# Three edits in one: tokens kept on chip and a split first norm in layer 0, five row blocks of layer 1's convolution on VectorE, and a regrouped softmax, selection and scatter in the experts

## The chip, the cores and the metric

The kernel runs on one core of a Trainium2 chip. The metric is the device time of one execution in microseconds (us). The engines are PE (TensorE), DVE (VectorE), ACT (ScalarE), POOL (GpSimd) and SP (SyncE), which issues all of this kernel's DMAs. Each engine works through its own instructions in program order, and waits on semaphores for the others.

## The reference, cut to what matters

The input `x` is [2, 56, 56, 128] in float32: two images (b) of 3136 tokens with 128 channels. Four layers follow one another.

```
x = x + ss2d0(groupnorm(x))            # layer 0: in_proj, 3x3 depthwise conv, SiLU, four selective scans, norm * SiLU(z), out_proj
x = four_heads(x)                      # layer 1: per head of 32 channels: layernorm, in_proj, 3x3 conv, SiLU,
                                       #   four selective scans, gated norm, out_proj; a head starts from the sum
                                       #   of the head before and its own chunk; then a final layernorm
t = t + attention(ln(t))               # layer 2
t = t + spectral_mixer(ln(t))
t = t + attention(ln(t))               # layer 3
t = t + experts(ln(t))

def experts(x):                        # 64 experts, K = 8 tokens for each expert and image
    probs = softmax(x @ gate_w.T + gate_b, axis=tokens)
    topv, topi = top_k(probs, 8)                   # per expert, along the tokens
    pooled = sum_k topv * x[topi]                  # one row for each expert
    h = gelu([pooled, 1] @ weight1)
    o = [h, 1] @ weight2
    out.at[topi].add(topv * o)                     # scattered back to the tokens
```

A depthwise convolution has nine taps for each channel, and each output row needs the row above and the row below.

## The kernel before, in words

The tokens are 28 blocks of 112 (`TP`, `NT`). `k.X` [112, 28, 2, 128] is the running activation, and stays in SBUF for the whole program. Channels lie in partitions in chunks of `CH` = 448 tokens (eight image rows), so there are seven chunks (`NCH`). Six large buffers `big` are used in turn by all layers; `pair` in the profile holds the first two, which layer 0 calls `y[0]` and `y[1]`.

**Layer 0** (`layer0`). Nine weight loads stand first in SP's queue. `norm(b)` (L574) loads the tokens of an image into a tile `xt` (L580), transposes them on PE (L99, in groups of four), evacuates by DVE and ACT in turn (L64, L68), takes statistics (L587, L589), sums over groups of four channels with a matmul by `grp` (L591, L598) and normalises (L603). The result is stored to DRAM in `kept` (L604). Both images are normalised before anything else. Then, for each image b, a loop over c = 0..7 calls `before`: chunk c of the norm is loaded back (`hin`, L645), projected on PE (L648) into zero-bordered images `pad0` and `pad1` (L649 on ACT), and the convolution of chunk c-1 is made by `conv_rows`. That has two forms: on PE as nine matmuls with diagonal matrices `diag` (L460, 18 instructions in the profile), or on DVE as one multiplication and eight multiply-adds (L464, L466). ACT applies SiLU (L467), and POOL writes a transposed copy (L468). Channel half 1 is always on DVE; half 0 is on PE except for c = 2 and 5. At c = 2, `scans.first` prepares the first group of the scan (projections L166, the step `keep` that stores its rows at L182, `fetch` of `whole` at L189, `spread` of `three` at L205); its two scratch areas lie in `y[0]` and `y[1]`. After the loop `scans.run` works through 512 scan steps per image. In the scan stages the order of the instructions is written out by hand; in all other stages a scheduler orders them and places the waits.

**Layer 1** (`Layer1`). Between two scans there is a transition: `after` closes a head, `before` opens the next for the same chunk c: `layernorm_tokens`, four transposes, projection (L844 into `pad`, L856 for the gate), convolution of chunk c-1 (c = 2, 4, 6 on DVE; 1, 3, 5, 7 on PE), gate. The first transition (from about 2769 us to 2914 us) has layer 0's `after` beside it; the three others follow each head. The PSUM pool `pcon1` has two buffers, which projections and PE convolutions share. The first step of the new scan needs `b` (a matmul by L364), `h` (L417 on DVE) and `a` (L339 on ACT).

**Experts** (`Experts.run`). `pr` holds the logits, experts of both images in the 128 partitions and tokens along the free dimension. DVE finds the eight largest (L1785), and marks them in a copy `sel` (L1788, match_replace). ACT takes the exponential with its sum (L1789), and scales by the reciprocal (L1791); DVE makes `sel` the probabilities at the marks and zero elsewhere (L1792). PE transposes `sel` (L1797), DVE multiplies by the layernorm's scale (L1801), and 56 matmuls pool the tokens (L1805). After the 64 experts (L1837, L1847, L1828) `oe` is bias plus outputs (L1868, L1869), and for each image and each four token blocks four matmuls with 64 rows scatter it back (L1876), DVE adds `X` into `xo` (L1881, three buffers), and SP stores it (L1882).

Of the kernel before, what the change touches and what calls it, by code (L numbers as in the profile page):

```python
# [21 lines left out]
B = 2  # L22
# [536 lines left out]
def layer0(k, d, big, follow):  # L559
# [3 lines left out]
    with ExitStack() as ctx:  # L563
        wp = ctx.enter_context(k.pool("w0"))
        W = {n: load(nc, wp, d["L0_" + n], "L0" + n) for n in (
            "in_w", "in_b", "taps", "conv_b", "dtb", "A", "Ds", "onw", "onb")}
        negative_exp(nc, W["A"])
# [6 lines left out]
        def norm(b, pools, G):  # L574

            ip, pp = pools
            hT = ip.tile([128, L], F32, name="hT")
            xt = ip.tile([TP, NT, C], F32, name="xt")
            for j in range(0, NT, 4):
                nc.sync.dma_start(  # L580
                    xt[:, j : j + 4], d["x"][b, TP * j : TP * (j + 4)].rearrange("(j p) c -> p j c", p=TP)
                )
            tokens_to_channels(k, pp, lambda c0: hT[:, c0 : c0 + CH], lambda j: xt[:, j, :])
# [22 lines left out]
        with ExitStack() as sctx:  # L606
# [11 lines left out]
            with k.pool("in0", 2) as ip, k.pool("pin0", 2, psum=True) as pp:  # L618

                grp = ip.tile([128, 32, 4], F32, name="grp0")  # L620
                nc.vector.tensor_reduce(grp[:, :, 0], k.ident.rearrange("p (g c) -> p g c", c=4), AX.X, ALU.add)
                nc.vector.tensor_scalar_mul(grp[:, :, 0], grp[:, :, 0], 0.25)
                for c in range(1, 4):
                    nc.vector.tensor_copy(grp[:, :, c], grp[:, :, 0])
                for b in range(B):
                    norm(b, (ip, pp), grp.rearrange("p g c -> p (g c)"))
# [13 lines left out]
            def before(b, pools, c, pads, diag):  # L640

                sp, pp = pools
                if c < NCH:
                    h = sp.tile([128, CH], F32, name="hin")
                    nc.sync.dma_start(h, kept[b, :, CH * c : CH * (c + 1)])  # L645
# [7 lines left out]
                if c > 0:  # L653
                    for ci in range(2):
                        conv_rows(
                            k, pools, pads[ci], diag, W["taps"][:, ci], W["conv_b"][:, ci : ci + 1], row[ci],
                            col[ci], c - 1, "DVE" if ci == 1 or c in (2, 5) else "PE",
                        )
# [41 lines left out]
            for b in range(B):  # L700
                with ExitStack() as bctx:
# [8 lines left out]
                    diagonals(k, diag, W["taps"][:, 0])  # L710
                    for ci in range(2):
                        pads.append(ip.tile([128, PAD, PAD], F32, name=f"pad{ci}"))
                        clear_border(nc, pads[ci])
                    for c in range(NCH + 1):
                        if b > 0 and c < NCH:
                            after(b - 1, (sp, pp, ip), c, *outs)
# [16 lines left out]
class Layer1:  # L733
# [85 lines left out]
    def before(self, head, pools, c, pad):  # L819
# [29 lines left out]
        if c > 0:  # L849
            conv_rows(  # L850
                k, (sp, vp), pad, self.diag, W["taps"], W["conv_b"], self.row, self.col, c - 1,
                "DVE" if c % 2 == 0 else "PE",
# [852 lines left out]
class Experts:  # L1705
# [6 lines left out]

    NE, NH, EC = 64, 512, 4
# [51 lines left out]
    def run(self, out):  # L1765
        k, nc, tc, X, W = self.k, self.k.nc, self.k.tc, self.k.X, self.W
        NE, NH, EC, pr = self.NE, self.NH, self.EC, self.pr
        with ExitStack() as ctx:
# [14 lines left out]
            with k.pool("e3t") as up, k.pool("pe3", 2, psum=True) as pp:  # L1783
                top = up.tile([128, 8], F32, name="top")
                nc.vector.max(top, self.tops.rearrange("p c n -> p (c n)"))  # L1785
                m = up.tile([128, 3], F32, name="m")
                nc.vector.tensor_scalar_mul(m[:, 0:1], top[:, 0:1], -1.0)
                nc.vector.match_replace(sel, top, pr, -3e38)  # L1788
                nc.scalar.activation(pr, pr, AF.Exp, bias=m[:, 0:1], accum_out=m[:, 1:2])  # L1789
                nc.vector.reciprocal(m[:, 2:3], m[:, 1:2])  # L1790
                nc.scalar.activation(pr, pr, AF.Copy, scale=m[:, 2:3])  # L1791
                nc.vector.scalar_tensor_tensor(sel, sel, -2e38, pr, ALU.is_lt, ALU.mult)  # L1792
                selT = up.tile([TP, NT, B, NE], F32, name="selT")
                for j in range(0, NT, 4):
                    ps = pp.tile([TP, 4, B, NE], F32, name="ps")
                    for i in range(4):
                        nc.tensor.transpose(  # L1797
                            ps[:, i].rearrange("p b e -> p (b e)"), sel[:, TP * (j + i) : TP * (j + i + 1)], k.ident
# [3 lines left out]
                ps = pp.tile([128, B, NE], F32, name="pp")  # L1802
                for b in range(B):
                    for j in range(NT):
                        nc.tensor.matmul(  # L1805
                            ps[:, b], lhsT=X[:, j, b, :], rhs=selT[:, j, b], start=j == 0, stop=j == NT - 1
                        )
                raw = up.tile([128, B, NE], F32, name="raw")
                nc.vector.tensor_copy(raw, ps)
                ps = pp.tile([128, B, NE], F32, name="pp")  # L1810
                nc.tensor.matmul(ps, lhsT=less, rhs=raw, start=True, stop=True)
                for b in range(B):
                    for e in range(EC):
                        k.evacuate(pooled[:, e::EC, 2 * e + b], ps[:, b, e::EC])
# [47 lines left out]
            oe = sp.tile([128, C], F32, name="oe")  # L1862
# [5 lines left out]
            nc.vector.tensor_copy(oe, pb)  # L1868
            nc.vector.tensor_tensor(oe, oe, every, ALU.add)  # L1869
            op = ctx.enter_context(k.pool("e3o", 3))  # L1870
            po = ctx.enter_context(k.pool("peo", 2, psum=True))
            for b in range(B):
                for j in range(0, NT, 4):
                    ps = po.tile([TP, 4, C], F32, name="po")
                    for i in range(4):
                        nc.tensor.matmul(  # L1876
                            ps[:, i, :], lhsT=sel[NE * b : NE * (b + 1), TP * (j + i) : TP * (j + i + 1)],
# [142 lines left out]
```

## Time and profile before

| what | before |
|---|---|
| median of three runs (all runs) | 9146.21 us (9146.21, 9135.08, 9156.23) |
| profiled execution: its time, its span | 9148.52 us, 9146.7 us |
| busy, share of the span | PE 88%, DVE 77%, POOL 69%, ACT 42% |
| mean granted TensorE clock | 0.947 |
| first scan instruction of layer 0, image 0 | 115.83 us |
| transitions into layer 1's heads 0 and 1: first scan instruction | 2914.59 us, 3648.01 us |
| experts: start of match_replace, last pooling matmul's result read | 8958.63 us, 8991.62 us |
| last scatter addition starts | 9142.44 us |

A line of the timeline has the start in us from the span's start, the duration in us, the engine, the line in the code, the operation, the tiles written and read with their shapes, and how many instructions are merged; in brackets stand the idle time before it and what ended it. A line of windows has, for a stretch of time, the busy time and the number of instructions of each engine, the granted clock of PE (1.00 is full speed) and the share and rate of the DMA engines. A PE matmul in float32 counts as two instructions, a PE transposition as one.

### The profile page before, as it was taken

The numbers are of one execution on the slowest core, as the hardware profiler recorded it, in microseconds if no ns is written. First come the engines' busy times: TensorE is split into PE (matmuls) and PEld (weight loads), VectorE is DVE, ScalarE is ACT, GpSimd is POOL, SyncE is SP. The second block draws the span as 40 slices with busy tenths as digits, with TensorE's granted clock in tenths as the row PEclk, the third lists the DMA queues.
The fourth block names the chain that finished last, engine by engine and source line by source line (L and its number), as shares of the span: only waits on it lengthen the run. The fifth ranks groups of instructions, "written<-read, shape, count | busy, mean of one in ns | idle before, by whom it ended". The sixth has DMA issues, their size and how long they took to land.

```text
span 9146.7 us, 93661 instructions
## 1 busy us (share of the span) xinstructions
PE 8045.3 (88%) x28769; PEld 4798.2 (52%) x28769; DVE 7065.7 (77%) x7533; ACT 3851.1 (42%) x6642; POOL 6343.6 (69%) x4065
## 2 busy tenths in 40 slices
PE   7888888888888888888888888699999999999998
PEld 3444445444445444444444444455688888874555
DVE  8999998999996997998899799611467677665442
ACT  4555555555555554554554555433211111114331
POOL 5999996999995997998899799566311111115551
PEclk9999999999998998998999899799999999999998
DMA  5666663676663995996788599100233333320003
GB/s 154 222 219 220 223 219 123 219 221 222 221 223 93 227 229 135 224 228 163 193 228 213 146 227 228 43 3 3 85 96 104 103 95 109 91 62 7 14 5 129
DMA packets 781377, 1364.55 MB, mean 149 GB/s; under 512 B 133213, under 2 KB 406494, under 8 KB 780842
## 3 DMA queue, kind: packets, MB, share of 16 engines
q1 hardware_dynamic: 780874, 1358.56, 52.8%
q8 instruction: 228, 3.74, 0.2%
q14 instruction: 275, 2.25, 0.1%
HBM read 1318.63 MB, written 39.60 MB: 148 GB/s over the span
## 4 chain that ended last, share of the span: by engine, by line
PE 46%; DVE 26%; issue 14%; ACT 7%; POOL 4%; DMA 2%; SPq 1%; DVEq 0%; POOLq 0%; ACTq 0%
DVE h L358 13%; PE cv L1548 13%; DVE h L417 8%; PE av L1059 6%; PE sc L1065 5%; PE acc L378 4%; PE pj L1662 4%; ACT a L339 3%; PE b L166 3%; PE pcv L460 2%; DMA c<-rows 1%; PE b L364 1%; POOL p L430 1%; POOL h L433 1%; PE acc L392 1%
## 5 line engine op out<-in xcount | busy, mean ns | idle before, releaser
L430 POOL TENSOR_TENSOR p<-h,c 128x784 f32<-128x784 f32 x2048 | 3754.3, 1856 | 115.9 <-DVE h L358 37.8
L358 DVE TENSOR_TENSOR_SCAN h<-a,state,h 128x784 f32<-128x784 f32 x1536 | 2788.3, 1837 | 48.6 <-ACT a L339 26.8
L378 PE MATMUL acc<-p,center 128*128 128x392 f32 x4096 | 1500.8, 500 | 16.0 <-POOL p L430 14.9
L378 PE MATMUL acc<-p,ident 128*128 128x392 f32 x4096 | 1494.3, 499 | 6.1 <-POOL p L430 6.0
L417 DVE TENSOR_TENSOR h<-du,b 128x784 f32<-128x784 f32 x1408 | 1332.5, 946 | 86.2 <-PE b L364 81.0
L339 ACT ACTIVATE a<-delta,L0A 128x784 f32<-128x784 f32 x1024 | 939.1, 918 | 974.3 <-DVE h L358 972.1
L339 ACT ACTIVATE a<-delta,L1A 128x784 f32<-128x784 f32 x1024 | 939.2, 917 | 911.9 <-DVE h L358 908.7
L364 PE MATMUL b<-three,sel 96*128 96x512 bf16 (+1 forms) x2816 | 730.4, 342 | 561.1 <-DVE h L417 456.6
L433 POOL TENSOR_TENSOR h<-du,b 128x784 f32<-128x784 f32 x640 | 1185.8, 1853 | 9.7 <-PE pcv L460 9.7
L378 PEld LDWEIGHTS acc<-p,center 128*128 128x128 f32 x4096 | 742.9, 193 | 529.3 <-POOL p L430 50.7
L378 PEld LDWEIGHTS acc<-p,ident 128*128 128x128 f32 x4096 | 745.4, 193 | 512.7 <-issue 26.8
L1078 POOL TENSOR_TENSOR total<-total,e 128x448 f32<-128x448 f32 (+1 forms) x644 | 735.6, 1142 | 325.1 <-ACT e L1067 285.7
L364 PEld LDWEIGHTS <-sel 96*128 96x128 bf16 x2816 | 282.1, 100 | 1231.9 <-issue 1052.9
L358 DVE TENSOR_TENSOR_SCAN h<-a,h 128x784 f32<-128x784 f32 x512 | 900.6, 1777 | 33.6 <-ACT a L339 23.2
L1561 DVE TENSOR_TENSOR u<-u,cv 128x512 f32<-128x512 f32 x1024 | 623.3, 679 | 326.8 <-PE cv L1548 325.5
L1592 POOL TENSOR_TENSOR u<-u,S 128x1024 f32<-128x1024 f32 x64 | 150.0, 2366 | 1042.7 <-DVE S L1561 1042.7
L1067 ACT ACTIVATE e<-sc 128x448 f32<-128x448 f32 (+1 forms) x700 | 377.4, 543 | 725.4 <-PE sc L1065 592.8
L1563 ACT COPY u<-cv 128x512 f32<-128x512 f32 x256 | 149.5, 587 | 827.2 <-PE cv L1548 773.5
L1662 PE MATMUL pj<-u,Wm 128*128 128x196 f32 (+8 forms) x1536 | 354.3, 384 | 5.7 <-DVE A L1668 5.7
L1065 PE MATMUL sc<-big 128*128 128x448 f32 (+1 forms) x700 | 323.2, 547 | 15.2 <-ACT e L1067 12.1
L1059 PE MATMUL av<-e,big 128*128 128x448 f32 (+1 forms) x700 | 320.8, 545 | 1.1 <-DVE e L1072 1.0
L1642 POOL TENSOR_TENSOR both<-mpm 128x512 f32<-128x512 f32 x32 | 40.6, 1270 | 391.2 <-DVE Wm L1698 271.7
(449 smaller groups left out, 11289.0 us busy)
## 6 DMA issues: line engine op xcount, KB each, us to landing
c<-rows SPq DMA_DIRECT2D x1024, 392.0 KB, 4.1
c<-rows SPq DMA_DIRECT2D x2048, 196.0 KB, 4.8
b<-rows SPq DMA_DIRECT2D x320, 392.0 KB, 4.6
b<-rows SPq DMA_DIRECT2D x640, 196.0 KB, 4.5
H<-raw SPq DMA_DIRECT2D x32, 1568.0 KB, 7.6
wC<-win SPq DMA_DIRECT2D x64, 576.0 KB, 6.3
w<-in_L_weight_dram SPq DMA_DIRECT2D x52, 512.0 KB, 5.6
wA<-win SPq DMA_DIRECT2D x64, 384.0 KB, 5.5
```

The lines of the kernel that those rows point to most:

```text
L339: self.k.nc.scalar.activation(x["a"], g["delta"][ci], AF.Exp, scale=self.w["A"](g["kd"], ci, x["n"]))
L358: self.k.nc.vector.tensor_tensor_scan(h, a, h, start, ALU.mult, ALU.add)
L364: self.k.nc.tensor.matmul(ps[:, c0:c1], lhsT=self.w["selB"](x["n"]), rhs=x["g"]["three"][:, c0:c1], start=True, stop=True)
L378: nc.tensor.matmul(job["acc"][:, i, 0:392], lhsT=self.w["sum"], rhs=x["p"][:, 392 * i : 392 * (i + 1)], start=False, stop=n == NS - 1,)
L417: nc.vector.tensor_tensor(one["h"], one["g"]["du"][one["ci"]], one["b"], ALU.mult)
L430: nc.gpsimd.tensor_tensor(now["p"], now["h"], now["c"], ALU.mult)
L433: nc.gpsimd.tensor_tensor(three["h"], three["g"]["du"][three["ci"]], three["b"], ALU.mult)
L1059: nc.tensor.matmul(acc, lhsT=V[b][:n, j, :], rhs=e[:n], start=j == 0, stop=j == NKT - 1)
L1065: nc.tensor.matmul(ps[:n], lhsT=keys[b][:, KT * j : KT * j + n], rhs=q, start=True, stop=True)
L1078: nc.gpsimd.tensor_tensor(total[:n], total[:n], e[:n], ALU.add)
L1548: self.k.nc.tensor.matmul(ps[:, b], lhsT=v[:, C * b : C * (b + 1)], rhs=h, start=i == 0, stop=i == len(terms) - 1)
L1662: nc.tensor.matmul(ps[:, lo - c0 : hi - c0], lhsT=Ws[f][:, eo, r, :], rhs=u[:, b, f, lo - a0 : hi - a0], start=f == 0, stop=f == 1,)
```

## The change

Layer 0: the tokens of image 0 are loaded straight into `X` ahead of the weights, those of image 1 after the weights. `norm` writes to `y[b]` instead of a tile of its own. Image 0's norm runs at the start of its loop, and its chunks are read from `y[0]` without the load; image 1's norm is called inside that loop at c = 2. `kept` is stored for both, as before. The convolution of half 0 of image 0 is on PE for all chunks; for image 1 it stays as it was. The diagonals are made after the pads.

Layer 1: the convolutions on DVE are those of c = 2 to 6 for head 0, and of c = 2, 4, 5, 6 for the other heads. So five row blocks leave PE for DVE: two in head 0, one in each other head.

Experts: the exponential goes to a tile of its own, `ex`, from the logits, so that it doesn't depend on the marks. The division by the sum goes into a diagonal matrix `shares`, by which PE multiplies while it transposes (a matmul in place of a transposition). The selection is made in seven pieces of 448. The pooling matmuls of a group follow its multiplication, in two accumulators. Four copies write `pooled` in place of eight. At the end, `oe` holds both images side by side with zeros elsewhere, so that one matmul with 128 rows and 256 columns serves both; the sums go into free weight buffers `w` of seven instead of the three `xo`.

```diff
+        def tokens(b):
+            for j in range(0, NT, 4):
+                nc.sync.dma_start(
+                    X[:, j : j + 4, b, :], d["x"][b, TP * j : TP * (j + 4)].rearrange("(j p) c -> p j c", p=TP)
+                )
+
+        tokens(0)
         W = {n: load(nc, wp, d["L0_" + n], "L0" + n) for n in (
             "in_w", "in_b", "taps", "conv_b", "dtb", "A", "Ds", "onw", "onb")}
+        tokens(1)
...
-            hT = ip.tile([128, L], F32, name="hT")
-            xt = ip.tile([TP, NT, C], F32, name="xt")
...
-            tokens_to_channels(k, pp, lambda c0: hT[:, c0 : c0 + CH], lambda j: xt[:, j, :])
+            hT = y[b]
+            tokens_to_channels(k, pp, lambda c0: hT[:, c0 : c0 + CH], lambda j: X[:, j, b, :])
...
-                    h = sp.tile([128, CH], F32, name="hin")
-                    nc.sync.dma_start(h, kept[b, :, CH * c : CH * (c + 1)])
+                    if b == 0:
+                        h = y[0][:, CH * c : CH * (c + 1)]
+                    else:
+                        h = sp.tile([128, CH], F32, name="hin")
+                        nc.sync.dma_start(h, kept[b, :, CH * c : CH * (c + 1)])
...
-                            col[ci], c - 1, "DVE" if ci == 1 or c in (2, 5) else "PE",
+                            col[ci], c - 1, "DVE" if ci == 1 or b == 1 and c in (2, 5) else "PE",
...
+                        norm(0, (ap, tp), groups)
+                    diagonals(k, diag, W["taps"][:, 0])
                     for c in range(NCH + 1):
+                        if b == 0 and c == 2:
+                            norm(1, (ap, tp), groups)
...
-                "DVE" if c % 2 == 0 else "PE",
+                "DVE" if c in ((2, 3, 4, 5, 6) if head == 0 else (2, 4, 5, 6)) else "PE",
...
+                ex = up.tile([128, L], F32, name="ex")
+                nc.scalar.activation(ex, pr, AF.Exp, bias=m[:, 0:1], accum_out=m[:, 1:2])
                 nc.vector.match_replace(sel, top, pr, -3e38)
-                nc.scalar.activation(pr, pr, AF.Exp, bias=m[:, 0:1], accum_out=m[:, 1:2])
-                nc.vector.reciprocal(m[:, 2:3], m[:, 1:2])
-                nc.scalar.activation(pr, pr, AF.Copy, scale=m[:, 2:3])
-                nc.vector.scalar_tensor_tensor(sel, sel, -2e38, pr, ALU.is_lt, ALU.mult)
+                nc.vector.reciprocal(share, m[:, 1:2])
+                shares = up.tile([128, 128], F32, name="shares")
+                nc.vector.tensor_scalar_mul(shares, k.ident, share)
...
+                for c in range(NCH):
+                    cs = slice(CH * c, CH * (c + 1))
+                    nc.vector.scalar_tensor_tensor(sel[:, cs], sel[:, cs], -2e38, ex[:, cs], ALU.is_lt, ALU.mult)
...
-                        nc.tensor.transpose(
-                            ps[:, i].rearrange("p b e -> p (b e)"), sel[:, TP * (j + i) : TP * (j + i + 1)], k.ident
+                        nc.tensor.matmul(
+                            ps[:, i].rearrange("p b e -> p (b e)"), lhsT=sel[:, TP * (j + i) : TP * (j + i + 1)],
+                            rhs=shares, start=True, stop=True,
                         )
...
+            for b in range(B):
+                rows = slice(NE * b, NE * (b + 1))
+                nc.vector.scalar_tensor_tensor(oe[rows, b], every[rows], share[rows], bias[rows], ALU.mult, ALU.add)
             po = ctx.enter_context(k.pool("peo", 2, psum=True))
+            for j in range(0, NT, 4):
+                w = wp.tile([128, self.PAIR], F32, name="w")
+                xo = w[:TP, 0 : 4 * B * C].rearrange("p (j b c) -> p j b c", b=B, c=C)
+                for i0 in range(0, 4, 2):
+                    ps = po.tile([TP, 2, B, C], F32, name="po")
+                    for i in range(2):
+                        ts = slice(TP * (j + i0 + i), TP * (j + i0 + i + 1))
+                        nc.tensor.matmul(ps[:, i], lhsT=sel[:, ts], rhs=oe, start=True, stop=True)
+                    nc.vector.tensor_tensor(xo[:, i0 : i0 + 2], X[:, j + i0 : j + i0 + 2], ps, ALU.add)
...
```

## The prediction

> **What bounds the kernel now.** I read the page first, then the stretches around each edited place as windows, then their timelines, and for the last place the chain of waits.
>
> ```profile
> PE 8045.3 (88%) x28769; PEld 4798.2 (52%) x28769; DVE 7065.7 (77%) x7533; ACT 3851.1 (42%) x6642; POOL 6343.6 (69%) x4065
> ```
>
> PE is busiest, but the change touches neither the scans nor the 64 experts, where most of that lies. It touches about 115 us at the start, 145 us before head 0, some 100 us before each later head, and two stretches of 20 to 35 us in the experts. Each has its own limit.
>
> ```profile
> 41.00:77.00 36.00, 28.52 (x51) 12.37 (x52) 23.75 (x35) 15.11 (x24) 6.50 (x6) 0.76 0.16 48
> 77.00:113.00 36.00, 32.60 (x86) 15.30 (x85) 32.95 (x48) 11.63 (x19) 10.31 (x9) 1.00 0.24 66
> ...
> 2820.00:2870.00 50.00, 43.95 (x204) 29.75 (x205) 20.66 (x37) 29.75 (x46) 18.16 (x20) 0.90 0.15 40
> 3600.00:3648.00 48.00, 42.56 (x123) 19.30 (x121) 22.89 (x39) 32.23 (x48) 15.88 (x18) 0.93 0.26 63
> ```
>
> Layer 0's start fills only once the chunks are there (DVE 23.75 of 36, then 32.95 of 36). In layer 1's transitions PE is busy nearly 90% and DVE under half.
>
> ```profile
> 38.31 8.89 SPq L645 DMA_DIRECT2D hin<-kept  x4
> 42.81 0.64 ACT L649 ACTIVATE pad<-pcv,L0in_b 128x448 f32<-128x448 f32 x1 [11.44 <-PE pcv L648]
> 102.44 9.90 DVE L466 SCALAR_TENSOR_TENSOR cv<-pad,L0taps,cv 128x448 f32<-128x448 f32 x15
> 115.83 3.47 DVE L358 TENSOR_TENSOR_SCAN h<-a,h 128x784 f32<-128x784 f32 x2 [0.23 <-ACT a L339]
> ...
> 3639.65 7.03 PE L460 MATMUL pcv<-pad,diag 128*128 128x448 f32 x18
> 3647.12 0.97 DVE L417 TENSOR_TENSOR h<-du,b 128x784 f32<-128x784 f32 x1 [4.49 <-PE b L364]
> ```
>
> The first pad comes at 42.81 after a trip through DRAM, with ACT idle for 11.44, and layer 0's first scan follows DVE's convolutions. In a head, DVE waits 4.49 for PE's `b`, which stands behind the last convolution on PE.
>
> ```profile
> 8963.41 2.91 ACT L1789 ACTIVATE pr<-pr,m 128x3136 f32<-128x3136 f32 x1
> 8969.58 3.43 DVE L1792 SCALAR_TENSOR_TENSOR sel<-sel,pr 128x3136 f32<-128x3136 f32 x1 [2.97 <-ACT pr L1791]
> 8973.06 3.84 PE L1797 MATMUL ps<-ident,sel 128*112 128x128 f32 x16 [16.19 <-DVE sel L1792]
> ...
> 9123.99 4.93 PE L1876 MATMUL po<-oe,sel 64*112 64x128 f32 x40 [0.38 <-DVE oe L1869]
> 9128.57 0.69 DVE L1881 TENSOR_TENSOR xo<-X,po 112x512 f32<-112x512 f32 x1 [0.83 <-DMA out_dram<-xo]
> 9138.65 3.75 PE L1876 MATMUL po<-oe,sel 64*112 64x128 f32 x16 [0.28 <-DVE xo L1881]
> ```
>
> At the experts' start DVE, ACT and PE work one after the other, PE idle for 16.19. At the end DVE waits for stores to free `xo`, and PE runs late at half pace (3.75 for 16).
>
> **Layer 0's start: gain 11.9.** Before, SP issues nine weights, then the tokens: first transposition 8.26, norm's statistics at 19.18, first pad 42.81. After, image 0's seven loads go first (0.73). They move 1.6 MB; at the 245 GB/s of the stretch from 26 to 41 they land by about 9.5, and the taps behind them by 10.4. DVE makes the second diagonal from the taps early in its order, so its evacuations (8.3 in sum) end at 18.7, 0.5 earlier only. The norm's chain of 5.4 ends at 24.1 and the first projection gives a pad at 25.7, 17.1 earlier: neither image 1's norm nor the trip through `kept` lies between. Seven issues of `hin` leave SP's queue. Later the path pays back. Image 1's norm now stands inside the loop: on DVE seven statistics at 0.62 and seven normalisations at 0.43 with their copies, against two convolutions (2 x 6.5) that go to PE. PE gets 2 x 7.0, and stands about 2 us behind that norm's statistics. On SP, seven stores of image 1 now stand ahead of the stores and loads of the scan's rows (68.35 before). I put these stores at 50 and the rows at 52, so they cost nothing with 1 to 2 us to spare; late, they push the rows back one for one. The last chunk's projection comes at 57.0 instead of 73.38. From there PE had 35.9 of convolutions and scan projections, and has 7.0 more: 100. SiLU 0.64, table load 1.28 and `a` 0.92 give the scan at 103.9 against 115.83. Bounds: -3, if PE's 14 us and the rows' delay eat the start, to 17, if nothing is paid back. I take the worked order.
>
> **Layer 1, head 0: gain 6 (0 to 12).** PE leaves out two blocks, c = 3 (2846.1 to 2853.1, behind which DVE waited 4.8 and 6.4) and c = 5 (9.6 with its wait), 16.7 in all, in a stretch where PE is busy 125.4 of 145. DVE gets 13 more; it has 67.9 busy and so 77 free, but each of the 18 instructions (0.45 to 0.74) can stand ahead of a layernorm link that PE waits for. ACT has two or three more table loads at 1.28, and near the end the wait from the last pad to the last statistics grows by about 4. 16.7 - 4 - 3.5 - 3 = 6; the upper end lets the last two be covered.
>
> **Layer 1, heads 1 to 3: 2.3 each, 6.9 (1.5 to 4.5 each).** The block c = 5 (7.06 at 3629.19) leaves PE. In ACT's new order the last pads come at 3631.2 and 3635.0, and the last PE block runs from 3635.4 to 3642.4 instead of 3639.65 to 3646.7, 4.3 earlier. But DVE ends block 4 at 3630.3 and then has 5 and 6, two by 6.47: 3643.2. Then `h` (0.97), the next `b` and `h`, and the scan at 3645.7 against 3648.01. DVE is late next, and half of what PE saves is lost to it.
>
> A rule speaks against relieving PE. The conv that began at 3594.36 in a stretch (3556 to 3600) granted 0.57 of the clock took 7.89 against 7.06 warm, though PE is counted busy there for 40.05 of 44. The Trainium skill, "TensorE: Matmul & The Clock Gate", Part 1 (The HAM clock gate), says that PE falls to half clock after some 3.4 us idle and needs as long to warm. By the rule alone a wholly cold block would be about twice 7.0, and the 11 blocks left on PE in the four transitions would cost some 6.2 more each. The windows say that PE stays above 70% busy even after giving up 7 of 48, so I put nothing in the sum and keep it as a rival.
>
> **Experts' start: gain 4.8 (3 to 8).** The exponential no longer waits for match_replace (3.41 at 8958.63); it has its table load at about 8958.7 and ends at 8962.9. The reciprocal is at 8963.2, `shares` 8964.2, DVE's first piece of 448 (a seventh of 3.43, some 0.5) at 8964.0, and ACT's scaling (2.91) is gone: PE starts at 8964.3, 8.8 earlier. It then pays: 28 transpositions (0.24 cold as in the 3.84 above, 0.15 warm) become matmuls of 128 columns by a full matrix. No row has these; the nearest, the experts' 128x128 sums, has 0.24 warm, so 0.47 cold: 28 x 0.1 to 0.2 = 4, of which the pooling hides none. The seven pieces stand ahead of the first `selT`. Result read at 8987.9 against 91.62, first expert at 8988.9 against 8993.7. Here too the clock rule speaks against the change: work moved to just after an idle PE is paid at half clock, and the row agrees (0.24 against 0.15).
>
> **Experts' end: gain 3.3 (1.5 to 5).** PE isn't relieved: 28 matmuls of 256 columns at 2 x 0.255 are 14.3, the old 112 instructions at the warm 0.123 are 13.8. What goes is the waiting: 9123.99 to 9142.4 was 18.4. With `oe` 0.3 later PE ends at 9138.6, DVE's last half 0.69 after, the last store issued at 9139.9 and landed 3.4 later (2.7 to 3.5 before): 9143.4 against 9146.7. Seven buffers `w` need no wait. The stores then want 221 GB/s, where the trace shows up to 254; at the lower end they bound it.
>
> Six more table loads on ACT in all. The trace has 1.28 each and the next activation at once (8962.11, then 8963.41): 7.7, while the skill's "ScalarE: Activation LUTs", What ACT_TABLE_LOAD costs, states about 2.66 for a switch with its drain: 16. The trace decides; by the rule the sum would be up to 8 less where ACT is on the path.
>
> **Sum.** 11.9 + 6 + 6.9 + 4.8 + 3.3 = 32.9. The profiled execution took 9148.5 (span 9146.7 and 1.8 around it), 2.3 above the median 9146.2. So 9115.6 against itself, and 9113 on the median. About 0.2% (18 us) is what a measurement can tell from no change: faster means under 9128.
>
> **The rivals.**
> - Layer 0 gives nothing (0.12): PE takes 14 us of blocks and norm 1, and becomes the bound. For it: PE already 32.6 of 36 from 77 to 113. Against: it had 0.76 of the clock and 7.5 us idle from 41 to 77. 21 saved: 9125.
> - Layer 1 gives nothing (0.11): every moved block's 6.5 on DVE replaces 7.0 of PE on the path, or the ACT order with its table loads does. For: in heads I already find DVE last. Against: DVE's share under half. 20 saved: 9126.
> - Layer 1 gives the whole 7.0 for each of five blocks (0.08): 35 instead of 12.9, 55 saved: 9091. DVE's 4.49 of waiting in the heads speaks for it, the two DVE blocks at the end against.
> - Slower (0.05): PE falls cold in layer 1's transitions. Place: the 11 remaining convolutions; price 6.2 each, up to 68. It outweighs the forecast's 32.9 from six cold blocks on; with all, 9146 - 33 + 68 = 9181. Against: the blocks shown last 7.0 to 7.1, with PE at nearly 90% around them; for: the one at 3594.36 with 7.89.
> - The change doesn't do what it says (0.01), as when image 1's loads hold back image 0's: 9146.
>
> **How the numbers follow.** The forecast has 0.63 and by its bounds reaches 9102 to 9126. Range: 9090 takes in the third rival, 9137 the first two with half of their bounds; left out are the slower cases and the far ends, under 0.2. Faster: 0.62 of the forecast, half of the first two rivals (0.115), 0.08 of the third: 0.82. Slower 0.04, the rest, 0.14, no change.
>
> **What would show it.** Right: first pad near 26, first scan near 104; heads' last PE block ending some 4 earlier with DVE's block the last before `h`, and the scan 2.3 earlier after the transition's start; the exponential beside match_replace and PE's first selection matmul 8.8 nearer to it; in the tail no DVE wait for DMA, and the last addition 3 nearer to `oe`. Wrong: first scan of layer 0 after 112, PE blocks of layer 1 over 8 us each, transitions as long as before, or rows of layer 0 stored after 60.

## The result, and the profile after

| | median | lowest to highest | runs |
|---|---|---|---|
| before | 9148.92 us | 9135.08 to 9156.23 | 5 |
| changed | 9101.38 us | 9098.37 to 9108.09 | 5 |

The ratio is 0.995 with a 95% interval of 0.9936 to 0.9965: 47 us faster, between 32 and 59. Run again beside 23 runs of the kernel before (median 9142.15), the changed kernel had 9109.6, ratio 0.9966 (0.9954 to 0.9978), 31 us faster. So 9113 was forecast, and 9101 and 9110 were measured. In the profiled executions of the two sets (9098.37 and 9111.66) one stage alone, the transition into head 0, differs by 14.1 us, with 27 and 61 us of it at half clock; the experiments take this up.

The first block of the profile's page is nearly unchanged, with 82 fewer instructions on PE and 35 more on DVE:

```profile
span 9096.6 us, 93496 instructions
## 1 busy us (share of the span) xinstructions
PE 7993.2 (88%) x28687; PEld 4765.5 (52%) x28687; DVE 7088.0 (78%) x7568; ACT 3854.8 (42%) x6644; POOL 6350.1 (70%) x4066
```

Both traces can be cut where a scan starts or ends, since each has the same 2048 scan instructions. A transition is the time from the last scan's end to the next scan's start. "Half" is the part of a stage, in us, in which the trace's clock records show PE at half clock. The forecast took the transition into head 0 from about 2769 us on; by the last scan's end it begins at 2762.2, and so lasts 152.4 and not 145.

| stage | before: us (half) | after: us (half) | difference | forecast |
|---|---|---|---|---|
| start to layer 0's first scan | 115.83 (18) | 102.45 (3) | -13.4 | -11.9 |
| layer 0, transition to image 1 | 130.11 (3) | 131.76 (7) | +1.7 | 0 |
| transition into head 0 | 152.40 (41) | 135.03 (27) | -17.4 | -6 |
| into head 1 | 97.39 (44) | 96.34 (51) | -1.1 | -2.3 |
| into head 2 | 99.89 (48) | 96.72 (51) | -3.2 | -2.3 |
| into head 3 | 97.02 (41) | 96.24 (51) | -0.8 | -2.3 |
| experts, marks to first expert matmul | 35.10 (21) | 29.13 (10) | -6.0 | -4.8 |
| from there to the first second-layer matmul | 10.48 (6) | 7.64 (0) | -2.8 | 0 |
| experts' loop and end | 142.51 (11) | 139.12 (2) | -3.4 | -3.3 |

The scans and layers 2 and 3, whose work is the same, make up the other 3.8 us of the 50.1 between the two spans.

**Layer 0's start**, from its timeline (start, duration, engine, line, what it writes and reads):

```profile
0.73 3.58 SPq L568 DMA_DIRECT2D X<-in_x_dram  x7
11.34 0.29 DVE L535 TENSOR_SCALAR diag<-ident,L0taps 128x128 f32<-128x128 f32 x1 [5.75 <-DMA L0taps<-in_L_taps_dram]
27.04 0.64 ACT L647 ACTIVATE pad<-pcv,L0in_b 128x448 f32<-128x448 f32 x1 [1.03 <-PE pcv L646]
53.76 0.32 SPq L182 DMA_DIRECT2D rows<-pair  x1
92.58 6.93 PE L460 MATMUL pcv<-pad,diag 128*128 128x448 f32 x18
102.45 3.47 DVE L358 TENSOR_TENSOR_SCAN h<-a,h 128x784 f32<-128x784 f32 x2
```

The first pad comes at 27.04 (25.7 was forecast, 42.81 before), after DVE has stood idle for 5.75 behind the taps. The rows go out at 53.76 (52), PE ends its last block at 99.5 (100), and the scan starts at 102.45 (103.9).

**Head 0**, by windows (length; busy us and instructions of PE, PEld, DVE, ACT, POOL; granted clock; DMA):

```profile
2746.00:2797.00 51.00, 44.79 (x223) 28.34 (x224) 34.73 (x68) 24.96 (x38) 26.11 (x33) 1.00 0.25 54
2797.00:2847.00 50.00, 41.12 (x230) 28.79 (x229) 33.75 (x60) 35.78 (x54) 28.18 (x26) 0.94 0.16 44
2847.00:2884.00 37.00, 22.04 (x66) 11.44 (x65) 19.69 (x35) 22.00 (x28) 11.20 (x10) 0.71 0.04 9
```

DVE is still far from full, and in this execution PE had full clock for the first 92.6 us of the transition, which begins at 2748.7.

**Head 1**, the end of its transition, and then the window from 3527 to 3568:

```profile
3605.85 8.71 PE L460 MATMUL pcv<-pad,diag 128*128 128x448 f32 x18
3614.40 0.50 PE L364 MATMUL b<-three,sel 96*128 96x512 bf16 x2
...
3612.54 0.96 DVE L417 TENSOR_TENSOR h<-du,b 128x784 f32<-128x784 f32 x1
3615.00 0.97 DVE L417 TENSOR_TENSOR h<-du,b 128x784 f32<-128x784 f32 x1 [1.50 <-PE b L364]
```

```profile
3527.00:3568.00 41.00, 38.88 (x165) 32.04 (x166) 20.16 (x58) 15.39 (x31) 24.20 (x26) 0.50 0.00 1
```

DVE's last block ends at 3612.6, where the forecast had it (93.1 from the transition's start against 92.6). But the last block on PE began 86.3 after the transition's start (84.8 in the forecast) and took 8.71 and not 7.0, so DVE waits for PE again, 1.50 before the last `h`. For 41 us PE is counted busy 95% and is granted exactly half its clock.

**Experts**, from the timeline of the changed kernel:

```profile
8920.68 3.41 DVE L1803 MATCH_REPLACE8 sel<-top,pr 128x3136 f32<-128x3136 f32 x1
8922.07 2.91 ACT L1802 ACTIVATE ex<-pr,m 128x3136 f32<-128x3136 f32 x1
8926.04 3.76 PE L1815 MATMUL ps<-shares,sel 128*112 128x128 f32 x16 [7.11 <-DVE shares L1806]
8949.81 4.46 PE L1857 MATMUL ph<-A,pooled 128*8 128x512 f32 x10 [0.35 <-DVE pooled L1832]
...
9077.73 13.42 PE L1903 MATMUL po<-oe,sel 128*112 128x256 f32 x56 [0.87 <-DVE oe L1894]
```

PE starts 5.36 after the start of the marks' instruction, match_replace (before: 14.43). The same ten expert matmuls were, in the kernel before:

```profile
8993.72 7.30 PE L1837 MATMUL ph<-A,pooled 128*8 128x512 f32 x10 [1.27 <-issue]
```

Here a second effect shows that the forecast had not: 4.46 in place of 7.30. At the end the 28 scattering matmuls run without a break, 13.42, where the old 112 instructions took 18.41. They start 0.5 later, as `oe` now takes the division by the sum too, and the program ends 4.7 after the last addition, 1.1 more than before.

### The profile page after: what moved, and what is told of

Its sections match the earlier page's. It is cut to its first block, busy times and chain, and to the rows that moved or that the text cites. A ratio compares the mean times of both kernels' runs of the same rounds, so it can differ in the third digit from the quotient of the medians.

```text
span 9096.6 us, 93496 instructions
## 1 busy us (share of the span) xinstructions
PE 7993.2 (88%) x28687; PEld 4765.5 (52%) x28687; DVE 7088.0 (78%) x7568; ACT 3854.8 (42%) x6644; POOL 6350.1 (70%) x4066
## 5 line engine op out<-in xcount | busy, mean ns | idle before, releaser
L430 POOL TENSOR_TENSOR p<-h,c 128x784 f32<-128x784 f32 x2048 | 3761.2, 1864 | 115.0 <-DVE h L358 33.1
L364 PE MATMUL b<-three,sel 96*128 96x512 bf16 (+1 forms) x2816 | 728.6, 341 | 563.9 <-DVE h L417 460.1
L364 PEld LDWEIGHTS <-sel 96*128 96x128 bf16 x2816 | 281.5, 100 | 1230.9 <-issue 1048.6
```

What stands on the lines that cost most here:

```text
L364: self.k.nc.tensor.matmul(ps[:, c0:c1], lhsT=self.w["selB"](x["n"]), rhs=x["g"]["three"][:, c0:c1], start=True, stop=True)
L430: nc.gpsimd.tensor_tensor(now["p"], now["h"], now["c"], ALU.mult)
```

## The experiments

Each kernel was timed in five rounds against the kernel before on the same chip. Kernels named with the same letter shared the chip and the runs of before. The profile of each gives one sample of every stage.

### The parts one by one

- `e1_layer0`: the kernel before with the hunks of layer 0 only.
- `e2_head0`: `"DVE" if c in ((2, 3, 4, 5, 6) if head == 0 else (2, 4, 6)) else "PE"`
- `e3_heads123`: `"DVE" if c in ((2, 4, 6) if head == 0 else (2, 4, 5, 6)) else "PE"`
- `e4_experts`: the hunks of the experts only.

> The kernel before with the changes of layer 0 alone. Theory A (the parts are independent, each worth what its own stage showed): first scan near 102.5, 13.4 earlier, image 1's transition up to 2 longer, everything behind it unchanged, so about 12 us faster than before. Theory B (the clock of TensorE decides as much as the moved work, and depends on where the windows of the clock fall, which the shorter start shifts): the stages of layer 1 and the experts, whose code is untouched here, also move by 3 us or more, with their time at half clock. By the prediction's own step 11.9 faster.

> The kernel before with the two blocks c = 3 and 5 moved to VectorE in head 0 alone. The prediction's step: 6 us, because ScalarE's extra table loads and VectorE's interleaved work cost some 10 of PE's 16.7. Theory A (the moved blocks alone make the gain seen): the transition into head 0 is about 17 shorter (152.4 to 135), whatever the clock does. Theory B (clock): PE's half-clock stretch at the transition's start, 13.7 us in the profile before and absent in the changed kernel though the instructions there are the same, is worth some 5.5 of the 17.4; where that stretch comes back the gain is about 12, and it varies from profile to profile without the edit.

> The kernel before with block c = 5 moved to VectorE in heads 1 to 3 alone. The prediction's step: 2.3 for each, 6.9 in all. Theory A: what the changed kernel showed, 1.0, 3.2 and 0.8, sum 5.0, because the last PE block, after PE has idled, runs partly at half clock (8.7 in place of 7.0) and holds back the b of the first step. Theory B: the order on VectorE alone bounds the end (last block ends with the PE block at full clock, 7.0): then each transition gains over 2. Time about 5 us faster, at the edge of what is measurable.

> The kernel before with the experts' changes alone. The prediction's step: 4.8 at the start and 3.3 at the end, 8.1. Theory A: as in the changed kernel, 12.2: 6.0 up to the first expert matmul, 2.8 more since the first ten expert matmuls run at full clock (4.5 in place of 7.3), because the shorter hand-over of the pooled sums no longer leaves PE idle, and 3.4 at the end. Theory B: the 2.8 is chance of the clock's windows: then here the first ten may take 7.3 again, and the gain is 9.

| kernel | median us (before 9144.17) | ratio, 95% interval | its own stages: us (half) |
|---|---|---|---|
| e1_layer0 | 9133.91 | 0.9986, 0.9978 to 0.9994 | first scan at 103.01 |
| e2_head0 | 9142.49 | 0.9995, 0.9987 to 1.0003 | head 0: 149.15 (55) |
| e3_heads123 | 9143.46 | 1.0, 0.9992 to 1.0008 | heads 1 to 3: 96.9, 95.0, 95.1 |
| e4_experts | 9135.96 | 0.9993, 0.9985 to 1.0002 | 29.23, 7.64, 139.14 |

Layer 0 and the experts behave in their own stages as in the changed kernel (12.8 and 12.1 saved). Heads 1 to 3 became shorter by 0.5, 4.9 and 1.9 beside the one profile of before, over 2 in only one of the three; the last PE block took 8.5 to 9.5, so half clock at the end, and not DVE's order alone, bounds them. Head 0 doesn't behave as in the changed kernel: 149.15, not 135. On each engine the order of the instructions in this transition is the same in both traces. The whole transition by windows, first of the changed kernel, then of e2_head0:

```profile
2748.70:2883.70 135.00, 106.23 (x512) 67.77 (x512) 85.17 (x159) 82.74 (x119) 62.50 (x66) 0.90 0.14 34
```

```profile
2754.00:2903.10 149.10, 119.65 (x512) 77.92 (x512) 85.29 (x158) 82.85 (x119) 62.60 (x66) 0.82 0.13 32
```

DVE, ACT and POOL do the same 85, 83 and 63 us of work, PE's 512 instructions take 13.4 longer, and the half-clock time is 55 instead of 27 us: 28 more, which at half pace are worth 14 us of a full-clock PE. That is the difference in length. Even unaltered stages moved so: in e1_layer0, head 0's transition, with the old code, took 156.25 (51).

The trace's clock records change only at multiples of 3.413 us, and the position of this grid against the program's start differs from execution to execution (0.24 to 3.13 in the profiles). The transition into head 0 begins with the grid's next boundary 0.4 after it in the changed kernel and in e3_heads123, and in neither is there a half-clock stretch in the first 50 us; in eleven other profiles, with the boundary at 0.59 to 1.30, there is one, 13.7 us long, that begins 10.8 to 11.5 in (the twelfth, g2_warm_all, has matmuls added there). So the theory that the moved blocks alone make 17 fell for head 0. The theory of the clock was right that the gain varies without the edit, but too small: it left a gain of 12 where the early stretch comes back, and 3.3 was seen, since half-clock stretches came later in the transition too.

The edit is best judged at like positions of the grid. With the boundary at 1.05 to 1.30, the transition takes 154.1 with the old blocks (3 profiles) and 147.3 with the new (7): 6.8. With the boundary at 0.4, it takes 148.8 and 135.0 (one profile each): 13.8.

### The changed kernel again, without the experts, and with another block moved

- `f1_again`: the changed kernel.
- `f2_layers01`: the changed kernel without the experts' hunks.
- `f4_blocks2346`: `(2, 3, 4, 6)` in place of `(2, 4, 5, 6)` for heads 1 to 3.

> The changed kernel once more, unaltered. Theory C (chance of the clock's windows): the boundaries of the 3.41 us windows fall anew in each run, so a longer list of runs scatters as that of the kernel before does, by some 25 us, its median lies nearer to the sum of the four parts measured alone (9144 less 10, 2, 1 and 8, that is 9123) than the 9101 of the first five runs, and the transition into head 0 takes over 140 in a profile in which TensorE spends over 40 us of it at half clock. Theory D (the parts help each other): the median stays at 9101 to 9105, and the head-0 transition near 135 with some 27 us at half clock.

> The changed kernel without the experts' changes. If the parts add (measured alone: 10 for layer 0, 2 and 1 for layer 1), some 9131 beside a kernel before of 9144; if layer 0's change and head 0's are worth more together than apart, as the changed kernel's first runs suggest, 9112 to 9117. In the heads each transition 2.2 shorter than before at 98.2 (mean of the four kernels profiled with the old heads), whatever the rest does.

> The changed kernel with block c = 3 instead of 5 on VectorE in heads 1 to 3. The prediction's step says that VectorE's blocks 5 and 6 at the end take back half of what PE saves; with 3 moved, VectorE is free at the end, and PE ends blocks 5 and 7 as late as before. If the end of the transition is set by PE's order and clock alone, the transitions last as in the changed kernel (96) or up to 3 less, for the block that leaves PE lies in the stretch where it runs at half clock (13 us a block instead of 7); if PE is then idle or at half clock for longer, they last 98 as before.

| kernel | median us (before 9142.15) | ratio, 95% interval | into heads 0, 1, 2, 3: us (half) |
|---|---|---|---|
| f1_again | 9109.6 | 0.9966, 0.9954 to 0.9978 | 149.1 (61), 97.1 (51), 97.0 (51), 96.9 (51) |
| f2_layers01 | 9112.93 | 0.997, 0.996 to 0.998 | 149.1 (61), 96.8 (51), 97.0 (51), 96.5 (51) |
| f4_blocks2346 | 9121.63 | 0.998, 0.9972 to 0.9987 | 142.8 (44), 100.8 (55), 100.0 (51), 102.2 (55) |

Neither theory for f1_again fits whole. Its head 0 took 149.1 with 61 us at half clock, as chance of the clock would have it, but the median stayed at 9110, where D had 9101 to 9105 and C 9123, and the runs scattered by 14 us, where C had 25. The four parts alone make 24 by their ratios, each known to 7, so 24 and 31 (20 to 42) don't contradict each other. f2_layers01 came out where its expectation put parts that help each other (9112 to 9117), 27 us faster (18 to 37) beside 17 for its three parts alone; these don't contradict each other either. That the parts help each other is not shown.

Over all profiles, the transitions into heads 1 to 3 last 98.2 with the old blocks (12 of them, 45 at half clock) and 96.2 with block 5 moved (15, 50 at half clock): 2.0 for each head, where 2.3 was forecast. Head 0 took 153.9 with the old blocks (5 profiles, 44 at half) and 145.8 with the new (8, 52 at half): 8.2, where 6 was forecast. The profiles of head 0 scatter by 4 to 5 us within each group, so 8 is known to some 5 only. The first pair's 17.4 lies well above it, and its changed half had the least half-clock time of all, 27 us.

f4_blocks2346 is slower: its transitions take 101 on average, longer than with no block moved. I expected 93 to 98. Without block 3, which PE otherwise has some 67 us in, a half-clock stretch of 10.2 us comes 71 to 74 in; with block 5 moved there is one of 6.8 at 81 to 84 instead. But half-clock time is only 53 against 50 us, worth 2 of the 5 us. The rest goes with the order: blocks 5 and 7 stand last on PE, as before the change, and DVE waits 4.49 for the `b` behind block 7, again as before. What delays those blocks further is not separated.

### Holding the clock by streaming useless columns

Why would an engine that is busy for 38.9 of 41 us be given half its clock? What PE does there is 166 weight loads, most of them followed by 2 or 64 columns. I summed the streamed columns per 3.413 us window of the clock, over all 14 profiles, at 0.87 ns a column in float32 at full clock (an instruction of 448 columns takes 0.39 us, as in the blocks of 18 in 7.03) and 0.49 in bfloat16 (0.50 for two of 512, L364), twice that at half clock. Of some 1540 windows after which the clock fell, 95% had streamed for less than 0.43 of their time; of some 32000 after which it stayed full, 95% for more than 0.53; of some 1540 after which it rose, none for less than 0.69. These shares are estimates, worked out from the columns and these times. By them it is the share of time in which columns stream that goes with the clock, window by window. These kernels test whether it is the cause:

```diff
         tiles = [slice(TP * i, TP * (i + 1)) for i in range(4)]
+        if head < 3:
+            for i in range((3, 2, 1, 1, 1, 1, 1)[c]):
+                nc.tensor.matmul(
+                    p.rearrange("p a j n -> p (a j n)")[:, 0:CH], lhsT=k.ident[:, 0:TP], rhs=y, start=True, stop=True
+                )
         for i, ts in enumerate(tiles):
             nc.tensor.matmul(p[:, 1, i], lhsT=gate[:, ts], rhs=self.outs[1], start=True, stop=True)
```

- `f3_warm`: this in the changed kernel.
- `g1_before_warm`: this in the kernel before.
- `g3_gap`: the changed kernel with `(3, 0, 0, 0, 0, 0, 0)`.
- `g2_warm_all`: f3_warm, and in the same way one matmul of 448 columns before each block's sums in the transition into head 0 (two before the first), seven at the experts' start.

> The changed kernel with ten useless matmuls of 448 columns on TensorE in each of the transitions into heads 1 to 3 (three before the first block's sums, two before the second's, one before each other; they write a PSUM tile that is overwritten at once). Theory E: the clock falls to half for 37 us at the start of these transitions not because TensorE is idle, it is counted busy for 95% of that time, but because its work there is weight loads with 2 or 64 columns each, so that columns stream through for under 0.4 of a window; columns streamed in between keep it at full clock. Then the half-clock time of a transition falls from 45 to 50 to under 30, and each transition gets 3 to 10 us shorter, although PE has 8 us more work at full clock. Rival F: the clock follows idle gaps alone; half-clock time stays at 45 to 50 and each transition gets 8 to 15 us longer.

> The kernel before with the ten useless matmuls of 448 columns in each of the transitions into heads 1 to 3, and nothing else of the change. If the clock decides these transitions by itself, they fall from 98.2 (mean with the old heads) to 88 to 92, about 25 faster in all. Held against the changed kernel with the same matmuls (87.6) this tells what moving block 5 to VectorE is worth when the clock is held: 2.3 each by the prediction's step (then 89.9 here), nothing (87.6) if the moved block's gain was itself only a matter of the clock, up to 7 if PE alone sets the end (94).

> The changed kernel with only three useless matmuls in each of the transitions into heads 1 to 3, all before the first block's sums, where PE waits 2.9 us for the gated block. If the idle gap is what makes the clock fall, filling it is enough: half-clock time under 30 and transitions near 88 as with all ten. If the small share of streamed columns in the weight-load-bound work behind it makes it fall, the clock falls a few us later all the same, half-clock time is over 35 and the transitions last 93 to 98.

> The changed kernel with the useless matmuls in heads 1 to 3, and more: in the transition into head 0 one of 448 columns before each block's sums (two before the first), and seven at the experts' start while TensorE waits for VectorE and ScalarE. By the theory that streamed columns hold the clock: head 0's half-clock time falls from 61 in the profiles at the common phase to under 45 and the transition from 149 to 138 to 145; from the marks to the first expert matmul 27 or less instead of 29.1 (or the 34.1 that one profile had at an unlucky phase). In all 5 to 20 faster than the kernel with heads 1 to 3 alone (9085). Rival: in head 0 PE is busy anyway and the eight more matmuls (6 us at full clock) cost what the clock gives; 149 stays or grows.

| kernel | median us | before | ratio, 95% interval | into heads 0, 1, 2, 3: us (half) |
|---|---|---|---|---|
| f3_warm | 9085.29 | 9142.15 | 0.9936, 0.9923 to 0.9948 | 149.1 (61), 89.7 (24), 86.5 (20), 86.5 (17) |
| g1_before_warm | 9126.58 | 9139.36 | 0.9984, 0.9978 to 0.9991 | 158.7 (55), 97.0 (27), 90.9 (14), 93.5 (20) |
| g3_gap | 9106.04 | 9139.36 | 0.9961, 0.9949 to 0.9974 | 142.6 (44), 96.0 (44), 95.3 (44), 97.2 (48) |
| g2_warm_all | 9092.24 | 9139.36 | 0.9946, 0.9934 to 0.9959 | 151.7 (55), 87.4 (24), 90.6 (24), 94.4 (38) |

The first 38 us of the transition into head 2, by windows, of f1_again, f3_warm and g3_gap:

```profile
4262.00:4300.00 38.00, 34.06 (x163) 28.71 (x163) 14.22 (x43) 12.07 (x25) 23.62 (x28) 0.62 0.00 1
```

```profile
4252.00:4290.00 38.00, 35.24 (x203) 23.80 (x204) 20.22 (x53) 16.88 (x32) 28.09 (x33) 1.00 0.01 1
```

```profile
4257.00:4295.00 38.00, 34.74 (x169) 27.74 (x170) 14.46 (x44) 11.81 (x25) 23.67 (x29) 0.68 0.00 1
```

With the useless matmuls PE works through 40 more instructions in the same 38 us, about half of them the added ones, at full clock. The timelines show that the sums then take 0.9 a group instead of 1.6 to 1.7, first in f1_again, then in f3_warm:

```profile
4276.03 1.60 PE L890 MATMUL pv<-mean,sq 128*112 128x2 f32 x8
4277.49 1.73 PE L888 MATMUL p<-outonb,pair 128*112 128x64 f32 x8
4279.02 1.70 PE L892 MATMUL p<-outonw,yc 128*112 128x64 f32 x8
```

```profile
4258.98 2.51 PE L889 MATMUL p<-big,ident 128*112 128x448 f32 x6 [1.69 <-ACT big L398]
4261.32 0.91 PE L893 MATMUL p<-outonb,pair 128*112 128x64 f32 x8
4262.07 0.90 PE L895 MATMUL pv<-mean,sq 128*112 128x2 f32 x8
4262.83 0.98 PE L897 MATMUL p<-outonw,yc 128*112 128x64 f32 x8
```

Filling the idle gap alone (g3_gap) delays the fall by some 4 us and no more. PE's idle time in these 38 us is nearly the same in the two (3.3 in g3_gap, 2.8 in f3_warm), and only f3_warm has full clock. So idle gaps alone don't explain the clock; streamed columns do, in these transitions. Whether the rows and columns of the array that a matmul fills count as well was not tested. f3_warm beats the changed kernel run beside it (9070 to 9087 against 9102 to 9116), and has the lowest ratio of all.

The added matmuls don't hold the clock every time. g2_warm_all has the same ones in heads 1 to 3, and there the third transition had 38 us at half clock and took 94.4. In the kernel before (g1_before_warm) the mean fell from 98.2 to 93.8, not to the 88 to 92 expected, and the program gained 15 us (8 to 20), not 25. In g2_warm_all the matmuls at the experts' start gave the stretch from the marks 28.8 with 3 us at half clock, hardly less than the 29.1 with 10 of f1_again; f3_warm had 34.1 with 21. Those before head 0's sums did not pay: 151.7 is no shorter than 149.1, so the rival stood there. The kernel was expected 5 to 20 us below f3_warm's 9085, and had 9092.

With the added matmuls in both kernels, block 5 moved to DVE seems worth more than the forecast: 93.8 in g1_before_warm (20 at half), 89.2 over f3_warm and g2_warm_all (24 at half), 4.6 a head, at the upper end of its range. The single transitions scatter by some 3 us, so this is not sure.

### The wait for the taps

```diff
+        W = {"taps": load(nc, wp, d["L0_taps"], "L0taps")}
         tokens(0)
-        W = {n: load(nc, wp, d["L0_" + n], "L0" + n) for n in (
-            "in_w", "in_b", "taps", "conv_b", "dtb", "A", "Ds", "onw", "onb")}
+        W |= {n: load(nc, wp, d["L0_" + n], "L0" + n) for n in (
+            "in_w", "in_b", "conv_b", "dtb", "A", "Ds", "onw", "onb")}
```

> The changed kernel with the load of the taps put ahead of the seven loads of image 0's tokens. In the changed kernel VectorE stands idle from 5.6 to 11.3 behind the diagonal that waits for the taps, with the evacuations of the transposed tokens queued behind it. By the prediction's step this wait is what keeps the norm from gaining more than 0.5 us: without it the norm's statistics end, and the first pad comes, 3 to 5 earlier (27.0 before), and the first scan up to 5 earlier than 102.3. Rival: PE's evacuations and ScalarE's share bound the norm, or PE is the bound later on: the pad comes earlier, but the scan under 1.

Median 9098.69, ratio 0.996 (0.9946 to 0.9973) to 9139.36, not to be told from the changed kernel. First pad 26.75 instead of 27.04, first scan 101.87, where the other eight profiles with the new start have 101.7 to 103.0. DVE's timeline says why:

```profile
2.40 1.34 DVE L535 TENSOR_SCALAR diag<-ident,L0taps 128x128 f32<-128x128 f32 x1 [0.41 <-DMA L0taps<-in_L_taps_dram]
12.49 0.16 DVE L526 TENSOR_REDUCE dsum<-L0Ds 128x2 f32<-128x8 f32 x1 [3.95 <-DMA L0Ds<-in_L_Ds_dram]
```

The diagonal no longer waits, but the next instruction in DVE's order that reads a late weight does, `Ds`. ACT waits in the same way for `A`, the load ahead of `Ds`, 5.50 until 12.30, and did so in the changed kernel too (5.38 until 11.83). Further evacuations stand behind both. One late weight took the place of another on DVE, another one stayed on ACT, and neither the step (3 to 5 earlier) nor its rival (PE's or ACT's share) had named them.

## Why the prediction was right, and where it was not

- **The total.** 32.9 was forecast, 47 and 31 were measured in two sets of runs. Sign and size are right. With averages over the profiles, in place of the first pair, the changed stages add up to some 38: layer 0 12.7 less 0.5 in image 1's transition, head 0 8.2, heads 1 to 3 6.0, the experts 5.0, 2.3 and 4.1. No term that was priced was far off, but in two of them errors cancel, as told below.
- **Layer 0.** The first scan starts at 115.0 on average in the five profiles with the old start and at 102.3 in the eight with the new one (without g4_taps_first): 12.7, where 11.9 was forecast. The chain went as written: rows at 53.8, the chunk's projection at 58.0 (57.0 in the forecast, where "the last chunk's" was a slip: it is chunk 3's), PE's end at 99.5. The -3 and the first rival (PE takes it all back) are excluded. From PE's end to the scan 3.9 was priced and 2.9 measured: the forecast's own three steps add up to 2.84, and 103.9 was a slip in the sum.
- **Head 0.** 6 forecast, 8.2 over 13 profiles, inside 0 to 12, but with the scatter and the dependence on the grid told above. The sum's parts are not shown one by one; of ACT's table loads four were added in the transition, where two or three were priced. The first pair's 17.4 would have misled.
- **Heads 1 to 3.** 2.0 each against 2.3, but with the wrong reason, so that the size is partly luck. The step "DVE is late next" failed: DVE ended where it was put (92.5 after the transition's start on average, 92.6 forecast), and PE was late again. In all 15 transitions with block 5 moved the last PE block took 8.5 to 9.5 (9.2 on average), where it had 7.03 in all 12 with the old blocks; it began at 85.7 and not 84.8; and DVE's last `h` waited 1.3 to 2.3 for PE. So PE paid 2.2 a head for the clock, which the sum had put at nothing. The slower rival had that mechanism, with its price per block too high (6.2 forecast, up to 2.5 seen; a wholly cold block would even be 7.0 more by its own words) and its reach too wide: of the three blocks in a head the first and the last ran over 8 us or close to it, but the first did so with the old blocks too, and the middle one stayed at 7.03. PE blocks over 8 us were named as a sign of being wrong, and for the last block the sign came.
- **The clock rule.** The Trainium skill, "TensorE: Matmul & The Clock Gate", Part 1 (The HAM clock gate), puts the fall of the clock down to some 3.4 us of idleness. I read PE's 70% and more of busy time as safe under it. Its two clocks and the length of its window agree with the trace (1 and 0.5, 3.413 us), but that reading doesn't: 41 us at half clock with PE counted busy for 38.9 of them. Relieving PE of wide work went with more half-clock time, some 5.5 us more in each of the three transitions (the 6.8 us stretch at the last block) and some 8 in head 0's, but not enough to turn the sign. By these numbers the sum would have needed some 2 us against the change in each head.
- **Experts' start.** 6.0 in the first pair, 5.0 over 13 profiles (without g2_warm_all), against 4.8. The 2.8 behind it (2.3 over these profiles) was left out: the ten expert matmuls ran at full clock. With the new code they took 4.46 in seven profiles of eight and 6.16 in f3_warm, with the old code 6.15 to 7.30 in all six. In the first pair PE idled 0.35 before them and not 1.27, with four copies of `pooled` instead of eight; that this shorter wait is what keeps the clock is not separated from the rest of the regrouping, and f3_warm shows that the gain is not sure.
- **Experts' end.** 3.4 in the first pair, 4.1 over 14 profiles, against 3.3. Part of this agreement is luck: PE's 28 matmuls took 13.4, priced at 14.3, `oe` was 0.5 later, priced at 0.3, and from the last addition's end to the program's end it took 4.7, priced at 4.1.

## What to carry to other kernels

Read the granted clock beside PE's busy share: an engine that is 95% busy with weight loads and few columns can be at half speed, as here for 41 us, and moving wide work away from it can make that worse. A few wide matmuls, even useless ones, can be worth more than they cost, if they are spread through the stretch and not only put into its gap; here they paid in heads 1 to 3 and not in head 0. And compare a stage over several profiles before its gain is put down to an edit: here one pair showed 17.4 for what is worth some 8.

## What the runs showed of the hardware

- In the 14 traces the clock steps between 1 and 0.5 on a grid of 3.413 us whose position differs from execution to execution. It goes with the share of time in which columns stream (estimated as above): 95% of the falls came after windows below 0.43, 95% of the windows that kept full clock were above 0.53, and no rise came below 0.69.
- A part of the scatter of this program's runs goes with it: over the 13 runs of e2_head0, time and mean granted clock have a correlation of -0.86, and 0.001 of the clock is about 2 us. Other changed kernels with 13 or more runs have -0.53 to -0.81, but the kernel before, over its 41, 23 and 25 runs, only -0.34 to -0.49. Even the scans of one image of layer 0, the same code in all, took 1252.5 to 1258.7, with 58 to 130 us at half clock.
- At the transition into head 0 most profiles had the grid at nearly the same position (the next boundary 0.4 to 0.6 after it in three, 1.05 to 1.31 in eleven), although it differs at the program's start. What brings it there was not tried.
